# Slot transposes between the second layer's tiles, and the base factors and Gelu's table behind the last routing

## The chip, the cores and the metric

The kernel runs on one core of one Trainium2 chip. The metric is the time of one execution on the device in microseconds (us). Before the change, three runs gave a median of 1468.1 us, from 1467.44 to 1471.71 us. One more execution was recorded by the hardware profiler; every view shown here comes from it.

The engines are named as in the profile: PE is TensorE (PEld its weight loads), DVE is VectorE, ACT is ScalarE, POOL is GpSimd, SP is SyncE, which only issues DMAs here. Each engine works through its own queue in the order in which the program puts instructions there.

## The reference

The input x has 4 batches of 1024 rows with 256 columns. The kernel computes one attention layer and one layer of experts, each followed by a layer norm over x plus the layer's output:

```
x = layernorm(x + attention(x))            # 16 heads of 16, magnitudes by softplus, angles by position
gates = softmax(x @ router_w + router_b)   # 8 experts
mask  = one_hot(top_k(gates, 2)).sum(1)    # two experts for each token
pos   = cumsum(mask, axis=0) - 1           # place of the token in its expert, over all 4096 tokens
valid = mask * (pos < 640)                 # an expert holds 640 tokens, the others get nothing from it
h = gelu(slots @ w1 + b1)                  # 640 x 256 -> 640 x 1024, for each expert
o = h @ w2 + b2                            # 640 x 1024 -> 640 x 256
x = layernorm(x + sum over experts of gates * valid * o)
```

## The kernel before, in words

**Attention and routing.** The attention of all four batches runs first, one pair of heads after another, and takes most of the time. Everything else of a batch, its routing among it, is cut into small pieces that are laid between the pieces of attention. The routing of one batch is a generator, `finish_batch` (L475 to L661); each `yield` ends a piece. It computes the layer norm's factor r (L495 to L502), normalizes rows (L511), transposes them on TensorE (L520), has ScalarE copy them (L525), multiplies by the router's weights (L531), forms gates, the two hot experts, the running count over tokens and the slot of each token (L555 to L629). After that it computes `again`, the factor of a second layer norm for tokens that get no expert's output ("base factors", L633 to L643), and then scatters each tile of 128 rows twice (once for each of the token's two experts) to the slots in DRAM, `slots_in`, by an indirect DMA that GpSimd issues (L652).

**The last routing.** For the last batch there is no attention left to lie beside. L1008 to L1038 run it in two halves of four tiles each, the generators `one` and `two` (with `rotate=True`), whose pieces are interleaved by hand. `one` is run to its end, its scatters included, then the rest of `two`. The base factors of `one` stand therefore on VectorE's and ScalarE's queues ahead of most of `two`.

**The experts.** L1188 to L1264 loop over eight experts; each has 640 slots, which are five tiles (ST = 5) of 128. The order of each engine's work is that of the program (`tc.manual_schedule()`). For each expert e:

- `slots_of(e + 1)` (L1054) queues the load of the next expert's slots on SP. The tile has two buffers, so this load starts when the last reader of the expert two before, the sum at L1163, is done.
- VectorE works out where results go (`tokens_of`, L1070), and the rows of the expert before are normalized (`normalized`, L1116) and sent out (L1176); the partial sums of earlier experts are gathered (L1153) and added (L1163). In the first expert only, `without_experts` (L1137) multiplies all rows by `again` and stores them.
- First layer, L1211 to L1227: eight chunks of the hidden size, each four matrix products on TensorE (L1215; in fp32 the trace shows two matmuls for each) and one Gelu on ScalarE (L1222).
- Second layer, L1228 to L1261: for each of the five tiles t, eight products (16 matmuls in the trace, L1234), then VectorE adds the bias (L1249), ScalarE scales by the gate (L1250), VectorE adds to the running rows (L1251), and GpSimd scatters the result (L1252).
- Ahead of tile t = 3 of the second layer, the slots of the next expert are transposed (`transposed`, L1061 to L1068): two TensorE transposes for each slot tile into PSUM and one ScalarE copy out of it. The PSUM tile `ps_t` has two buffers (L1045), so the transposes of the third slot tile need the copy of the first. The transposed slots `slots_t` have two buffers too.
- After the second layer, the weights of expert e + 2 are queued on SP (L1264).

ScalarE needs a table for its functions. The program loads the one for Sin at L120 and the one for Ln and Exp at L204 by name; the loads for Gelu and for the Sqrt of the last expert are put ahead of the first use by the compiler.

Of the kernel before, what the change touches and what calls it, by code (L numbers as in the profile page):

```python
# [14 lines left out]
AF = mybir.ActivationFunctionType  # L15
ALU = mybir.AluOpType
# [5 lines left out]
EPS = 1e-5  # L22
# [6 lines left out]
def kernel(  # L29
# [18 lines left out]
    nc = tc.nc  # L48
    B, S, DIM = x.shape
    E, _, HID = w1.shape  # L50
    HD = 16
    NT = S // P
# [8 lines left out]
    ST = CAP // P  # L61
# [23 lines left out]
    again = keep.tile([P, B * NT], F32, name="again")  # L85
# [16 lines left out]
    with ExitStack() as actx:  # L102
# [206 lines left out]
        xts, qks, oss, ots, stats = {}, {}, {}, {}, {}  # L309
# [165 lines left out]
        def finish_batch(b, rotate=False, lo=0, n=NT):  # L475


            mv = stats[b][:, lo : lo + n, :]
# [8 lines left out]
            def t1(name):  # L487
                return some(name, (NT,))[:, lo : lo + n]
# [5 lines left out]
            r, v, t = t1("ln_r"), t1("ln_v"), t1("ln_t")  # L494
# [134 lines left out]
            nc.vector.tensor_reduce(  # L629
                held[:, tiles, DIM : DIM + 2].rearrange("p t k -> p k t"), both, AX.X, ALU.add  # L630
            )

            more = again[:, b * NT + lo : b * NT + lo + n]  # L633
            nc.vector.tensor_tensor(v, r, r, ALU.mult)
            nc.vector.tensor_tensor(v, v, mv[:, :, 1], ALU.mult)
            nc.vector.tensor_scalar(v, v, EPS, None, ALU.add)
            nc.scalar.activation(more, v, AF.Ln)
            nc.scalar.activation(more, more, AF.Exp, scale=-0.5)
            yield
            nc.vector.tensor_tensor(t, more, more, ALU.mult)  # L640
            nc.vector.tensor_tensor(t, t, v, ALU.mult)
            nc.vector.tensor_scalar(t, t, -0.5, 1.5, ALU.mult, ALU.add)
            nc.vector.tensor_tensor(more, more, t, ALU.mult)  # L643
            for st in range(n):
                if st:
                    yield
                t = b * NT + lo + st
                if not rotate:

                    nc.vector.tensor_copy(scatter_idx[:, :, t], to[:, :, st])  # L650
                for k in range(2):
                    nc.gpsimd.indirect_dma_start(  # L652
                        out=scatter_views[2 * t + k],
                        out_offset=bass.IndirectOffsetOnAxis(
                            ap=scatter_idx[:, k, t : t + 1], axis=0
                        ),
                        in_=held[:, t, :],
                        in_offset=None,
                        bounds_check=SLOTS - 1,
                        oob_is_err=False,  # L660
                    )  # L661

        zero = aconst.tile([P, ROW], F32, name="zero")
        nc.gpsimd.memset(zero, 0.0)
# [174 lines left out]
        def run(pieces):  # L839
            next(pieces, None)  # L840
# [21 lines left out]
        for b in range(B):  # L862
# [10 lines left out]
            second = ((6, 4), (6, 6), (7, 0), (7, 2))  # L873
# [21 lines left out]
        with tc.manual_schedule():  # L895
# [48 lines left out]
            n = 0  # L944
# [14 lines left out]
        with tc.manual_schedule():  # L959
            for n in range(NS):  # L960
                u, c = divmod(n, NT)
                b, p = divmod(u, NU)
                if c == 0:
                    if u + 2 < B * NU:
                        load_qk(u + 2)
                    elif u + 2 - B * NU < 2:
                        e = u + 2 - B * NU
                        experts[e] = expert_weights(e)
                v, k = divmod(n + 1, NT)
                v, k = v + 1, 2 * k  # L970
# [30 lines left out]
                if b > 0 and (p, c) in FINISH:  # L1001
                    if b not in finishing:
                        finishing[b] = finish_batch(b - 1)
                    next(finishing[b], None)
# [3 lines left out]
        with tc.manual_schedule():  # L1008
            b, n = B - 1, NT // 2
            normalize(B * NU - 1, rotate=True)  # L1010
            for i in range(2):
                turn_back(b, 1, i, rotate=True)
            for j in range(2):
                project(b, 1, j, rotate=True)
                statistics(b, j)
            one, two = (finish_batch(b, rotate=True, lo=lo, n=n) for lo in (0, n))
            run(one)
            project(b, 1, 2, rotate=True)
            for _ in range(3):
                run(one)  # L1020
            project(b, 1, 3, rotate=True)
            for j in range(2, 4):
                statistics(b, j)
            for _ in range(3):
                run(one)
            run(two)
            for _ in range(2):
                run(one)
            run(two)
            for _ in range(4):  # L1030
                run(one)
            run(two)
            for _ in range(3):
                run(one)
            for _ in range(n):
                run(one)
            for _ in two:
                pass  # L1038


    with ExitStack() as mctx:
# [146 lines left out]
        with tc.manual_schedule():  # L1188
            for t in range(ST):
                transposed(0, tiles[0], t)  # L1190
            for e in range(E):
                w1_sb, w2_sb = experts.pop(e)
                s_sb, s_t = tiles.pop(e), s_ts.pop(e)
                if e + 1 < E:
                    tiles[e + 1] = slots_of(e + 1)
                if e == 0:
                    for q in range(7, 3, -1):
                        without_experts(q)
                w, to = tokens_of(e, s_sb)
                others = others_of(e, s_sb, w, to)  # L1200
                row = next(others)

                if before:
                    b_row, b_to = before
                    normalized([b_row[:, t, :] for t in range(ST)], f"e_{e}")
                next(others, None)
                if before:
                    for t in range(ST):
                        sent(b_row, b_to, t)
                h_t = m2.tile([P, HC, CAP], F32, tag="h", name=f"h_{e}")  # L1210
                for c in range(HC):  # L1211
                    ps = ps_h.tile([P, 2, 512], F32, tag="h", name=f"hp_{e}_{c}")
                    for k in range(KC):
                        for i in range(2):
                            nc.tensor.matmul(  # L1215
                                ps[:, i, 0:half],
                                w1_sb[:, k, c * P : (c + 1) * P],
                                s_t[:, k, i * half : (i + 1) * half],
                                start=(k == 0),
                                stop=(k == KC - 1),  # L1220
                            )
                    nc.scalar.activation(  # L1222
                        h_t[:, c, :].rearrange("p (i n) -> p i n", i=2),
                        ps[:, :, 0:half],
                        AF.Gelu,
                        bias=b1_sb[:, e, c : c + 1],
                    )  # L1227
                for t in range(ST):  # L1228
                    if e + 1 < E and t == ST - 2:
                        for i in range(ST):  # L1230
                            transposed(e + 1, tiles[e + 1], i)
                    ps = ps_o.tile([P, DIM], F32, tag="o", name=f"op_{e}_{t}")
                    for c in range(HC):
                        nc.tensor.matmul(  # L1234
                            ps,
                            h_t[:, c, t * P : (t + 1) * P],
                            w2_sb[:, c, :],
                            start=(c == 0),
                            stop=(c == HC - 1),
                        )  # L1240
                    if e == E - 1:
                        nc.vector.scalar_tensor_tensor(
                            row[:, t, :], ps, w[:, t : t + 1], row[:, t, :], ALU.mult, ALU.add
                        )
                        normalized([row[:, t, :]], f"e_{e}_{t}", by_scalar=True)
                        sent(row, to, t)
                        continue
                    o_sb = m4.tile([P, DIM], F32, tag="o", name=f"o_{e}_{t}")
                    nc.vector.tensor_tensor(o_sb, ps, b2_sb[:, e, :], ALU.add)  # L1249
                    nc.scalar.activation(o_sb, o_sb, AF.Identity, scale=w[:, t : t + 1])  # L1250
                    nc.vector.tensor_tensor(row[:, t, :], row[:, t, :], o_sb, ALU.add)  # L1251
                    nc.gpsimd.indirect_dma_start(  # L1252
                        out=y_views[e * ST + t],
                        out_offset=bass.IndirectOffsetOnAxis(ap=to[:, 1, t : t + 1], axis=0),
                        in_=o_sb,
                        in_offset=None,
                        bounds_check=2 * N - 1,
                        oob_is_err=False,
                    )
                    if e == 0 and t < 4:  # L1260
                        without_experts(3 - t)  # L1261
                before = row, to
                if e + 2 < E:
                    experts[e + 2] = expert_weights(e + 2)  # L1264
# [68 lines left out]
```

## Time and profile before

| | us |
|---|---|
| median of three runs | 1468.1 |
| the profiled execution, as timed | 1469.84 |
| its span, first to last instruction | 1468.0 |
| PE busy | 1372.4 (93%) |
| DVE busy | 917.8 (63%) |
| ACT busy | 728.6 (50%) |
| POOL busy | 410.2 (28%) |
| last attention product ends | about 1104 |
| first transposes of expert 0's slots | 1157.26 |
| first layer of expert 0 starts | 1160.05 |
| first layer of expert 7 starts | 1421.09 |

The mean granted clock of TensorE is 0.97 of full speed over the span.

How to read the views. A line of a timeline has the start in us, the duration (of a merged group, its sum of busy time), the engine, the line of the kernel, the operation, what is written and read, the shape, and how many instructions are merged (x64). In square brackets stands the idle time of the engine just before, and the event that ended it: `[0.93 <-issue]` means that the engine stood for 0.93 us and the profile shows no other instruction that released it. A line of the waits has the waiting engine and line, what it waited for, then the total in us, the number of times and the longest. In the slices of the page each digit is the busy share of a fortieth of the span, in tenths; PEclk is the granted clock in the same way. Ends of matmuls are modelled, so starts are the safer numbers.

### The profile page before, as it was taken

What the parts mean: (1) busy time and instruction counts of PE and PEld (TensorE: products, weight loads), DVE (VectorE), ACT (ScalarE), POOL (GpSimd) and SP (SyncE); (2) the same over time, 40 slices, a digit from 0 to 9 for tenths busy, and PEclk for the clock granted to TensorE, in tenths of its full rate; (3) what the DMA queues carried; (4) which work ended last, traced back from release to release, by engine and by line L of the source; (5) the groups of instructions that cost most, each with busy time, mean ns of one, the idle gap of its engine ahead of it and who ended that gap; (6) DMA issues with size and microseconds to landing.
All of it is one profiled execution on the core that took longest, in us unless ns stands there. A gap on an engine that the chain in (4) does not pass through costs nothing. (4 is left out here: it accounts for less than half of the span.)

```text
span 1468.0 us, 24361 instructions
## 1 busy us (share of the span) xinstructions
PE 1372.4 (93%) x9314; PEld 860.1 (59%) x9314; DVE 917.8 (63%) x1990; ACT 728.6 (50%) x944; POOL 410.2 (28%) x436
## 2 busy tenths in 40 slices
PE   5899999999999999999999999999994599999996
PEld 3455556555655565656556555555543377777775
DVE  6767766667877766787766677787715243333334
ACT  5365666565556656555664754655462222222221
POOL 5640043340002646000064520000402224434432
PEclk8799999999999999999999999999996699999998
DMA  7856367374344646453474542243210454333211
GB/s 234 262 161 186 99 189 201 89 226 119 108 120 137 190 128 212 122 153 88 116 216 134 151 135 63 71 105 84 76 58 7 131 181 154 107 115 130 72 40 43
DMA packets 107315, 191.23 MB, mean 130 GB/s; under 512 B 19633, under 2 KB 56178, under 8 KB 107072
## 3 DMA queue, kind: packets, MB, share of 16 engines
q1 hardware_dynamic: 96192, 167.80, 39.6%
q0 software_dynamic: 9888, 20.01, 4.4%
q10 hardware_dynamic: 1120, 1.87, 0.4%
q8 instruction: 73, 1.20, 0.4%
q14 instruction: 42, 0.34, 0.1%
HBM read 119.32 MB, written 73.63 MB: 131 GB/s over the span
## 5 line engine op out<-in xcount | busy, mean ns | idle before, releaser
L692 DVE TENSOR_REDUCE nm<-s 128x1 f32<-128x512 f32 x1024 | 644.6, 683 | 231.7 <-PE s L688 217.3
L737 ACT ACTIVATE pt<-st 128x1024 f32<-128x1024 f32 x512 | 496.2, 1021 | 392.7 <-PE st L730 375.8
L688 PE MATMUL s<-qk 128*128 128x512 f32 x1024 | 390.7, 440 | 23.7 <-DVE nm L692 12.1
L715 PE MATMUL st<-qk 128*128 128x512 f32 x1024 | 308.9, 401 | 4.4 <-ACT pt L737 3.4
L751 PE MATMUL av<-pt,va 128*32 128x256 f32 x4096 | 275.6, 386 | 0.5 <-ACT pt L737 0.5
L688 PEld LDWEIGHTS s<-qk 128*128 128x128 f32 x1024 | 179.9, 191 | 136.6 <-DVE nm L692 58.2
L715 PEld LDWEIGHTS st<-qk 128*128 128x128 f32 x1024 | 182.8, 189 | 68.1 <-ACT pt L737 33.2
L751 PEld LDWEIGHTS av<-pt,va 128*32 128x32 f32 x4096 | 107.2, 109 | 108.2 <-issue 63.0
L652 POOL DMA_INDIRECT slots_in<-held,scatter_idx x64 | 62.6, 977 | 306.0 <-DVE scatter_idx L650 225.1
L390 POOL TENSOR_TENSOR soft_q<-y_q,soft_q 128x512 f32<-128x512 f32 x14 | 17.9, 1279 | 448.0 <-ACT soft_q L386 448.0
L1234 PE MATMUL op<-w,h 128*128 128x256 f32 x640 | 140.6, 379 | 0.0
L1215 PE MATMUL hp<-slots_t,w 128*128 128x320 f32 x512 | 139.8, 434 | 0.0
L1234 PEld LDWEIGHTS op<-w,h 128*128 128x128 f32 x640 | 121.1, 190 | 17.0
L730 PE MATMUL st<-mt,ones_r 2*128 2x512 f32 x1024 | 130.1, 498 | 0.7 <-ACT mt L708 0.7
L1215 PEld LDWEIGHTS hp<-slots_t,w 128*128 128x128 f32 x512 | 97.7, 191 | 39.9 <-ACT slots_t L1068 0.3
L730 PEld LDWEIGHTS st<-mt,ones_r 2*128 2x128 f32 x1024 | 49.2, 182 | 90.0 <-issue 88.6
L1222 ACT ACTIVATE h<-hp,b_sb 128x640 f32<-128x640 f32 x64 | 50.8, 793 | 85.3 <-PE hp L1215 73.0
L1249 DVE TENSOR_TENSOR o<-op,b_sb 128x256 f32<-128x256 f32 x35 | 14.8, 424 | 103.7 <-PE op L1234 99.8
L1250 ACT ACTIVATE o<-o,w 128x256 f32<-128x256 f32 x35 | 17.8, 507 | 109.1 <-DVE o L1249 100.3
L1252 POOL DMA_INDIRECT y_rank<-o,rows x35 | 35.6, 1016 | 109.3 <-ACT o L1250 61.5
L1176 POOL DMA_INDIRECT out_dram<-row,rows x40 | 41.3, 1033 | 44.8 <-DMA out_dram<-row,rows 14.3
L463 DVE TENSOR_TENSOR held<-po,held 128x512 f32<-128x512 f32 x32 | 22.1, 690 | 41.8 <-PE po L455 41.8
(210 smaller groups left out, 1038.3 us busy)
## 6 DMA issues: line engine op xcount, KB each, us to landing
qk<-embed_q SPq DMA_DIRECT2D x248, 128.0 KB
qk<-embed_k SPq DMA_DIRECT2D x124, 256.0 KB
embed_k<-parts_k SPq DMA_DIRECT2D x64, 256.0 KB
w<-in_w_dram SPq DMA_DIRECT2D x16, 1024.0 KB
embed_q<-parts_q SPq DMA_DIRECT2D x56, 256.0 KB
y_rank<-zero SPq DMA_DIRECT2D x8, 1024.0 KB
tab_k<-table SPq DMA_DIRECT2D x14, 512.0 KB
tab_q<-table SPq DMA_DIRECT2D x12, 512.0 KB
```

What stands on the lines that cost most here:

```text
L652: nc.gpsimd.indirect_dma_start(out=scatter_views[2 * t + k], out_offset=bass.IndirectOffsetOnAxis(ap=scatter_idx[:, k, t : t + 1], axis=0) ...
L688: nc.tensor.matmul(ps, qk[:, 2 * h, lo : lo + P], qk[:, 2 * h + 1, j * HS : (j + 1) * HS], start=True, stop=True,)
L692: nc.vector.tensor_reduce(nms[u][:, j, i, s : s + 1], ps, AX.X, ALU.max, negate=True)
L715: nc.tensor.matmul(ps[:, f, :], qk[:, 2 * h + 1, c * P : (c + 1) * P], qk[:, 2 * h, f * HS : (f + 1) * HS], start=True, stop=False,)
L730: nc.tensor.matmul(tiles[h][:, f, :], ones_r[rows, :], mts[u][rows, :], start=False, stop=True,)
L737: nc.scalar.activation(pt, tiles[h], AF.Exp)
L751: nc.tensor.matmul(av[32 * s : 32 * (s + 1), cols], va[f][:, c, 2 * p + h, :], pt[h][:, s // 2, cols], start=(c == 0 and n == 0), stop=(c ...
L1176: nc.gpsimd.indirect_dma_start(out=out_views[t], out_offset=bass.IndirectOffsetOnAxis(ap=to[:, 0, t : t + 1], axis=0), in_=row[:, t, :], i ...
L1215: nc.tensor.matmul(ps[:, i, 0:half], w1_sb[:, k, c * P : (c + 1) * P], s_t[:, k, i * half : (i + 1) * half], start=(k == 0), stop=(k == KC ...
L1222: nc.scalar.activation(h_t[:, c, :].rearrange("p (i n) -> p i n", i=2), ps[:, :, 0:half], AF.Gelu, bias=b1_sb[:, e, c : c + 1],)
L1234: nc.tensor.matmul(ps, h_t[:, c, t * P : (t + 1) * P], w2_sb[:, c, :], start=(c == 0), stop=(c == HC - 1),)
L1252: nc.gpsimd.indirect_dma_start(out=y_views[e * ST + t], out_offset=bass.IndirectOffsetOnAxis(ap=to[:, 1, t : t + 1], axis=0), in_=o_sb, in ...
```

## The change

Three edits. First, the ten transposes for the next expert no longer stand in one group ahead of tile 3. Slot tile 0 is transposed ahead of t = 1, slot tile 1 ahead of t = 2, slot tile 2 ahead of t = 3, and slot tiles 3 and 4 ahead of t = 4. Second, the base factors become a generator of their own, `second_factors`. For the batches that lie beside attention the order stays what it was. For the two halves of the last batch it runs behind the scatters: that of `two` when `two` is run out, that of `one` after it. Third, the table for Gelu is loaded by name right after that.

```diff
@@ finish_batch
-            more = again[:, b * NT + lo : b * NT + lo + n]
-            nc.vector.tensor_tensor(v, r, r, ALU.mult)
-            nc.vector.tensor_tensor(v, v, mv[:, :, 1], ALU.mult)
-            nc.vector.tensor_scalar(v, v, EPS, None, ALU.add)
-            nc.scalar.activation(more, v, AF.Ln)
-            nc.scalar.activation(more, more, AF.Exp, scale=-0.5)
-            yield
-            nc.vector.tensor_tensor(t, more, more, ALU.mult)
-            nc.vector.tensor_tensor(t, t, v, ALU.mult)
-            nc.vector.tensor_scalar(t, t, -0.5, 1.5, ALU.mult, ALU.add)
-            nc.vector.tensor_tensor(more, more, t, ALU.mult)
+            second = second_factors(b, lo, n, r, v, t)
+            if not rotate:
+                next(second)
+            yield
+            if not rotate:
+                next(second, None)
             for st in range(n):
...
+            if rotate:
+                yield
+                for _ in second:
+                    pass
+
+        def second_factors(b, lo, n, r, v, t):
+            more = again[:, b * NT + lo : b * NT + lo + n]
+            nc.vector.tensor_tensor(v, r, r, ALU.mult)
+            nc.vector.tensor_tensor(v, v, stats[b][:, lo : lo + n, 1], ALU.mult)
+            nc.vector.tensor_scalar(v, v, EPS, None, ALU.add)
+            nc.scalar.activation(more, v, AF.Ln)
+            nc.scalar.activation(more, more, AF.Exp, scale=-0.5)
+            yield
+            nc.vector.tensor_tensor(t, more, more, ALU.mult)
+            nc.vector.tensor_tensor(t, t, v, ALU.mult)
+            nc.vector.tensor_scalar(t, t, -0.5, 1.5, ALU.mult, ALU.add)
+            nc.vector.tensor_tensor(more, more, t, ALU.mult)
@@ the last routing
             for _ in two:
                 pass
+            run(one)
+            nc.scalar.preload_act_table_set("gelu_and_others")
@@ the experts' second layer
                 for t in range(ST):
-                    if e + 1 < E and t == ST - 2:
-                        for i in range(ST):
+                    if e + 1 < E and t > 0:
+                        for i in (t - 1,) if t < ST - 1 else (t - 1, t):
                             transposed(e + 1, tiles[e + 1], i)
```

## The prediction

> **What bounds the kernel now.** I read the page's slices first, then the timeline of TensorE alone in the expert stage, then TensorE's waits, then all engines' timeline where the two stages meet. In the slices:
>
> ```profile
> PE   5899999999999999999999999999994599999996
> PEclk8799999999999999999999999999996699999998
> ```
>
> One slice is 36.7 us. TensorE is full everywhere except at the start, in slices 30 and 31 (about 1101 to 1175 us: the last routing), and at the very end. So time is won only by taking something out of TensorE's own queue, or by shortening the chain through slices 30 and 31. TensorE's timeline of one expert (e = 2), with the first line of the next one:
>
> ```profile
> 1235.09 17.39 PE L1215 MATMUL hp<-slots_t,w 128*128 128x320 f32 x64
> 1252.32 10.52 PE L1234 MATMUL op<-w,h 128*128 128x256 f32 x48
> 1262.68 0.60 PE L1067 MATMUL st<-ident,slots 128*128 128x128 f32 x4
> 1264.21 0.71 PE L1067 MATMUL st<-ident,slots 128*128 128x128 f32 x4 [0.93 <-issue]
> 1265.11 0.44 PE L1067 MATMUL st<-ident,slots 128*128 128x128 f32 x2 [0.19 <-ACT slots_t L1068]
> 1265.38 7.07 PE L1234 MATMUL op<-w,h 128*128 128x256 f32 x32
> 1272.29 17.39 PE L1215 MATMUL hp<-slots_t,w 128*128 128x320 f32 x64
> ```
>
> Read the starts. First layer 17.23 us (1252.32 - 1235.09); three tiles of the second layer 10.36, so 3.45 a tile; the ten transposes of the next expert's slots 2.70 (1265.38 - 1262.68); two more tiles 6.91. Together 37.20. In the 2.70 us TensorE stands twice. Its waits from 1178 to 1438 us are only these:
>
> ```profile
> PE st L1067 <- ACT slots_t L1068: 6.7, 12, 0.9
> PE st L1067 <- issue: 1.1, 2, 0.9
> ```
>
> Fourteen waits, two for each of seven experts: the transposes write a ring of two PSUM tiles (ps_t), ScalarE empties them, and its copies stand behind the second-layer output of the tile before. Now the meeting of the stages, in the timeline of all engines:
>
> ```profile
> 1126.62 0.22 DVE L629 TENSOR_REDUCE held<-both 128x8 f32<-128x64 f32 x1
> 1126.76 0.15 DVE L634 TENSOR_TENSOR ln_v<-ln_r 128x4 f32<-128x4 f32 x1
> ...
> 1127.83 0.16 DVE L640 TENSOR_TENSOR ln_t<-again 128x4 f32<-128x4 f32 x1 [0.51 <-ACT again L638]
> ...
> 1128.51 0.97 DVE L511 TENSOR_SCALAR held<-held,mv,ln_r 128x256 f32<-128x256 f32 x2
> 1129.06 1.17 PE L520 MATMUL x1p<-ident,held 128*128 128x128 f32 x4 [3.05 <-DVE held L511]
> 1130.27 0.58 ACT L525 COPY xt<-x1p 128x512 f32<-128x512 f32 x1 [2.00 <-PE x1p L520]
> ...
> 1141.40 0.97 POOL L652 DMA_INDIRECT slots_in<-held,scatter_idx  x1 [4.34 <-DVE ln_v L635]
> ```
>
> From L634 on, VectorE works at the second factors of the first half, which nobody needs yet, while L511 of the second half stands behind them, and TensorE and ScalarE wait for L511. The last line is the first of the second half's eight scatters; GpSimd had been idle for 4.34 us. (The line names L635, but L635 began at 1141.22 and lasted 0.16; L629, done at 1141.12, is 0.28 earlier, the same distance as 1126.84 to 1127.12 in the first half. L629 releases it.) Eight scatters, the load of slots and the first transposes at 1157.26 follow without slack.
>
> **Part 1, the transposes between tiles.** Nothing is added to or removed from TensorE's work: ten transposes stay, in groups of 2, 2, 2 and 4 in place of one group of 10. What goes is the waiting. How long is a group that doesn't wait? In the unstalled first four, narrow windows of the same timeline give starts of 1262.68, 1262.79, 1262.90 and 1263.01: 0.11 each. Entering costs nothing: the two tiles behind give 6.91 / 32 = 0.216 us a matmul, and 48 of them from 1252.32 end where the transposes start. Leaving: the last transposes start at 1265.11 and 1265.27, the matmul after them at 1265.38, so 0.27 for a group of two that came out of a wait. Low bound 10 x 0.11 = 1.10, high bound 5 x 0.27 = 1.35; I take 1.20, nearer to the unstalled row, since these groups come behind full matmuls. Saved: 2.70 - 1.20 = 1.50 for each of six experts and 2.65 - 1.20 = 1.45 for e = 0 (1188.33 to 1190.98), 10.45 in all; bounds 9.4 and 11.1.
>
> Do the waits come back? The ring: transposes of slot tile 2 (at t = 3) need the copy of tile 0, two tiles earlier; those of tile 4 (at t = 4) need the copy of tile 2. That copy comes behind o_2 on ScalarE: VectorE's add ends some 0.6 us after the tile's matmuls, the scale takes 0.51, the copy 0.37, so about 1.6 us after the tile, and the transposes come 3.9 us after it: 2.3 us of cover. The last two copies (two of 0.37) end about 1.9 us into the last tile and the next first layer wants them 3.9 us in. On ScalarE a copy now stands before o_t of each tile; it waits only for transposes at the head of that tile's 3.45 us, so it is through before o_t can start. Uncovered, a late copy costs its lateness.
>
> The slots must be there 6.9 us earlier than now (t = 1, not t = 3). The load is issued when L1163 of the expert before is through: for e = 3 at 1219.73, used at 1262.68. Only the load used in e = 1 is close: issued at 1199.35 among two weight loads; the gathers name it as landed by 1209.17, and t = 1 would want it at 1218.57. Cover 9.4 us; at most it costs what is missing, once.
>
> **Part 2, the second factors.** Off the path of the first half go L634 to L643: seven VectorE instructions and two on ScalarE with 0.51 us of waiting. L511 can start when L629 is issued through, about 1126.81 in place of 1128.51: 1.70 us. ScalarE's Ln and Exp (1127.36, 1127.59), ahead of the first x1p copy, go too; that copy no longer decides. From L511 on each link waits for the one before, so the shift reaches 1141.40. There GpSimd's idle 4.34 us less 1.70 stays positive, so the first half's scatters don't become the limit. I take 1.70, bounds 1.2 and 1.9 (VectorE's row pair took 0.97 here and 0.73 beside an idle GpSimd).
>
> The moved steps issue no DMA and pass no queue of SP or GpSimd. They land behind the second half's own factors, which end at 1142.86, 1141.2 when shifted; 1.8 us more ends at 1143.0. The next VectorE work, L1142, waits for a scatter until 1145.99, 1144.3 shifted: cover 1.3 us, and beyond it only stores of x1 that nobody waits for.
>
> TensorE's clock may take some back. The windows say 0.50 before 1160 and 0.76 in 1160 to 1163: half speed until about 1161.44. That is why the first expert's first layer took 17.92 in place of 17.23. The Trainium skill (TensorE: Matmul & The Clock Gate, Part 4) holds that transposes don't count as busy, which would keep the first layer cold for a whole window of about 3.4 us (Part 1) and cost 1.7 us; the trace had 0.69, 4.2 us after the first transpose, so the row decides. The same Part 1 has the window free-running: by it the warm end falls 3.4 to 6.8 us after the start, 0.3 to 2.0 us lost, -0.4 to +1.3 against now. Shifting the start has no preferred sign; I take 0.
>
> **Part 3, the table.** One load moves from before the first Gelu to behind the last Exp:
>
> ```profile
> 1160.30 0.37 ACT L1068 COPY slots_t<-st 128x256 f32<-128x256 f32 x1 [0.35 <-PE st L1067]
> 1160.69 1.28 ACT L1222 ACT_TABLE_LOAD   x1
> 1163.10 0.79 ACT L1222 ACTIVATE h<-hp,b_sb 128x640 f32<-128x640 f32 x1 [1.13 <-PE hp L1215]
> ```
>
> The skill (ScalarE: Activation LUTs, What ACT_TABLE_LOAD costs) prices a switch at 2.66 us, load and drain; by it I would take off up to 2.66. But the Gelu stood 1.13 us idle after the load, for TensorE: the load lies beside the matmuls, and its removal is worth 0. In its new place ScalarE is idle for 15.92 us, so it costs 0 too; uncovered it would be 1.28. The copies and the Identity between the Gelus cause no load now (the page's groups have four loads in the kernel), so none is added.
>
> **Sum.** 10.45 + 1.70 = 12.15. The profiled span goes from 1468.0 to 1455.85, its execution (1469.84, 1.84 around the span) to 1457.7. The median of runs, 1468.1, is 1.74 below that execution: 1456.0.
>
> **Rivals.** *Switching costs more.* Each exit from transposes exposes the next weight load (0.19): four exits, 0.76 an expert, 5.3 in all: 1461.3. Against it: the exit above took 0.11. *The clock or VectorE eats part 2*: 1457.7. *The wait moves*: transposes find slots or ring not ready and lose what they saved; only part 2 is left, 1466.4. For it: ScalarE's in-order queue; against it the covers above. *Slower, the clock of the dense stage*: the breaks go, TensorE runs without any pause from the first expert on, and its granted clock drops. From 1178 us on some 265 us are TensorE's; the gain is gone at 265 x (1/c - 1) = 12.15, c = 0.956. At 0.93, which the window of 30 to 200 us shows, it costs 19.9: 1475.9. Against it: the windows of 200 to 600 us are 99% busy at 1.00.
>
> **How the numbers follow.** Forecast 0.76; dearer switches 0.10; part 2 lost 0.08; wait moved 0.04; clock 0.02. The forecast's own range: at best 11.1 + 1.9 + 0.4 = 13.4, and the lowest run before lies 0.7 under its median, 1454.0; at worst 9.4 + 1.2 - 1.3 = 9.3, 1458.8. The range 1453.5 to 1460.0 takes in it and the third case, and leaves out some 0.18 (the dearer switches, the wait, the clock, and a little below). A measurement here tells apart about 0.3%, 4.4 us: faster by more holds the first three cases, 0.94; within it the moved wait, 0.04; slower 0.02.
>
> **What would show it.** Expert period 35.7 in place of 37.20, the second layer's starts 3.45 apart plus 0.22 to 0.27; no wait of L1067 on slots_t but the first expert's; L511 of the second half at about 1126.8, first transposes at about 1155.6; one table load near 1143 and none before the Gelu. Wrong if TensorE shows a new wait for slots or st between 1180 and 1440, if the first-layer or op spacing grows (clock), or if the chain at 1126 turns out to be set by another link.

## The result, and the profile after

Six runs of the changed kernel gave a median of 1454.74 us (1452.07 to 1456.68), six of the kernel before 1467.77 (1464.69 to 1471.71). The ratio is 0.9905, with a 95% interval from 0.9893 to 0.9917: 13.9 us faster, between 12.2 and 15.7. The medians differ by 13.0. The profiled execution took 1455.47 us with a span of 1453.6, 14.4 under the span of before.

The slices of the page after:

```profile
PE   5899999999999999999999999999996399999996
PEclk8899999999999999999999999999998599999998
```

A slice is now 36.3 us. The hole is still there, in slices 30 and 31, and the rest is as full as before. What changed inside the full part shows in TensorE's timeline of the same expert, e = 2 (the transposes are L1082 now, the second layer L1249):

```profile
1228.77 17.39 PE L1230 MATMUL hp<-slots_t,w 128*128 128x320 f32 x64
1246.00 3.62 PE L1249 MATMUL op<-w,h 128*128 128x256 f32 x16
1249.45 0.38 PE L1082 MATMUL st<-ident,slots 128*128 128x128 f32 x2
1249.67 3.62 PE L1249 MATMUL op<-w,h 128*128 128x256 f32 x16
...
1260.48 0.60 PE L1082 MATMUL st<-ident,slots 128*128 128x128 f32 x4
1260.91 3.62 PE L1249 MATMUL op<-w,h 128*128 128x256 f32 x16
1264.37 17.39 PE L1230 MATMUL hp<-slots_t,w 128*128 128x320 f32 x64
```

No line has square brackets: nothing waits. A group of two takes 0.22 us from its start to the next matmul (1249.67 - 1249.45), the group of four 0.43. The expert takes 35.60 in place of 37.20. The view of TensorE's waits from 1176 to 1430 us, two lines before, is empty, and the windows of the same stretch give a clock of 1.00 and 35.60 us of busy TensorE in each 35.60.

The view of the waits shows less than this: 0.93 + 0.19 = 1.12 us for the group of e = 2 before, where the starts give 1.60 (2.70 less 1.10). There the fourth transpose started at 1263.01 and counts as busy until 1263.28, so part of a stall is counted as work. The starts tell the whole price.

At the meeting of the stages, in the timeline of all engines:

```profile
1125.76 0.22 DVE L629 TENSOR_REDUCE held<-both 128x8 f32<-128x64 f32 x1
1125.90 0.73 DVE L511 TENSOR_SCALAR held<-held,mv,ln_r 128x256 f32<-128x256 f32 x2
...
1126.45 1.09 PE L520 MATMUL x1p<-ident,held 128*128 128x128 f32 x4 [1.30 <-DVE held L511]
...
1138.07 0.97 POOL L646 DMA_INDIRECT slots_in<-held,scatter_idx  x1 [1.88 <-DVE ln_v L666]
```

L511 starts 0.14 us after the start of L629 (1.89 before), and GpSimd's idle time ahead of the second half's scatters falls from 4.34 to 1.88. The first slot transposes start at 1153.96, 3.30 earlier than before. Not all of that is the edit's, as the runs below show.

The moved factors of the first half did not run where I had put them. In the same timeline (L665 to L674 are the factors, L1157 the scaling of finished rows that each wait for a scatter):

```profile
1139.47 0.15 DVE L665 TENSOR_TENSOR ln_v<-ln_r 128x4 f32<-128x4 f32 x1
...
1142.80 0.35 DVE L1157 TENSOR_SCALAR held<-held,again 128x256 f32<-128x256 f32 x1 [3.18 <-DMA slots_in<-held,scatter_idx]
1143.07 0.15 DVE L666 TENSOR_TENSOR ln_v<-ln_v,mv 128x4 f32<-128x4 f32 x1
...
1145.17 1.28 ACT L1053 ACT_TABLE_LOAD   x1
...
1147.66 0.16 DVE L674 TENSOR_TENSOR again<-again,ln_t 128x4 f32<-128x4 f32 x1
```

They ran on VectorE between the rows of L1157, which each wait for a scatter, and so end at 1147.82 and not at 1143. In kernel.py all seven of the first half's stand ahead of the first L1157; nothing on record says what put them between. Nobody waits for them: ScalarE still idles 8.25 us between the table load and the first copy of slots.

### The profile page after: what moved, and what is told of

Read it like the earlier page. It is cut to its first block, busy times and chain, and to the rows that moved or that the text cites. A ratio compares the mean times of both kernels' runs of the same rounds, so it can differ in the third digit from the quotient of the medians.

```text
span 1453.6 us, 24361 instructions
## 1 busy us (share of the span) xinstructions
PE 1367.7 (94%) x9314; PEld 859.4 (59%) x9314; DVE 921.3 (63%) x1990; ACT 727.5 (50%) x944; POOL 411.2 (28%) x436
## 5 line engine op out<-in xcount | busy, mean ns | idle before, releaser
L1249 PE MATMUL op<-w,h 128*128 128x256 f32 x640 | 144.1, 379 | 0.0
L1249 PEld LDWEIGHTS op<-w,h 128*128 128x128 f32 x640 | 119.4, 190 | 15.9
L396 POOL TENSOR_TENSOR e_k<-soft_k,tab_k 128x512 f32<-128x512 f32 x28 | 35.4, 1286 | 46.3 <-DMA tab_k<-table 45.8
```

What stands on the lines that cost most here:

```text
L1249: nc.tensor.matmul(ps, h_t[:, c, t * P : (t + 1) * P], w2_sb[:, c, :], start=(c == 0), stop=(c == HC - 1),)
```

## The experiments

**Theory.** Part 1 is the removal of TensorE's stalls in the group of ten, 1.6 us an expert; part 2 is VectorE's queue; the table is worth nothing. **Rivals.** The table or the granted clock gave part of it; or the ring of PSUM buffers is not what the transposes waited for.

The attention stage alone moves by several us from execution to execution: its last weighted values start between 1095.71 and 1104.86 in the twelve profiles. A timed ratio carries that along, so for effects of 1 or 2 us I measured stretches inside the profiles. In us: A, from that start to the first half's L629; B, from there to the first slot transposes; C, to the first layer of expert 0; D, that layer; H, how long of D the granted clock stood at half, by the clock's records in the trace; E, the mean period of experts 1 to 6. From the first layer of expert 7 to the end of the span it is 46.9 in all twelve.

| kernel | A | B | C | D | H | E |
|---|---|---|---|---|---|---|
| before | 23.66 | 30.64 | 2.79 | 17.92 | 1.39 | 37.20 |
| changed | 23.37 | 28.20 | 2.80 | 18.05 | 1.65 | 35.60 |
| e1 transposes only | 23.05 | 29.96 | 2.80 | 17.97 | 1.49 | 35.60 |
| e2 factors only | 22.95 | 28.24 | 2.80 | 17.52 | 0.58 | 37.20 |
| e3 table only | 23.38 | 29.99 | 2.80 | 18.89 | 3.34 | 37.20 |
| e4 changed, no table | 23.04 | 28.25 | 2.80 | 19.12 | 3.80 | 35.60 |
| e5 copies first | 23.35 | 28.21 | 2.80 | 18.35 | 2.26 | 36.52 |
| e6 one buffer | 23.04 | 28.24 | 5.10 | 19.66 | 4.91 | 36.96 |
| e7 one each | 23.38 | 28.31 | 5.11 | 18.78 | 2.69 | 35.60 |
| e8 rows early | 23.10 | 26.75 | 2.80 | 17.79 | 1.14 | 35.60 |
| e9 changed, again | 23.39 | 28.20 | 2.80 | 17.87 | 1.29 | 35.60 |
| e10 rows early, again | 22.96 | 27.47 | 2.80 | 17.90 | 1.36 | 35.60 |

D less half of H is 17.21 to 17.23 in eleven of the twelve. The twelfth is e7, with 17.44: its D also holds the two transposes ahead of t = 0, 0.22.

**e1, the transposes alone.** The kernel before with

```diff
-                    if e + 1 < E and t == ST - 2:
-                        for i in range(ST):
+                    if e + 1 < E and t > 0:
+                        for i in (t - 1,) if t < ST - 1 else (t - 1, t):
```

> Only the transposes are spread; the base factors and the table stay as before. If TensorE's waits in the group of ten were the cost: expert period 35.60 as in the changed kernel, no wait of the transposes after the first expert, time 11.0 to 11.2 us under before. If a good part of the gain came from the last routing or the table, it is under 9. The Gelu's table load stands again ahead of the first Gelu and the Gelu's wait for TensorE after it is about 1.1.

Ratio 0.9896 (0.9873 to 0.9919), median 1452.75. Column E is the changed kernel's, B is not. The ratio makes 15.2 us, from 11.9 to 18.6, a little beyond the 11.0 to 11.2 that I expected; the runs of before beside it spread from 1459.85 to 1473.51, and the stretches (9.63 in the six periods, and 1.55 in the first expert's second layer) give 11.18. Part 1 needs nothing of the other two.

**e2, the factors alone.** The kernel before with the generator `second_factors` behind the scatters and `run(one)` at the end; no load by name, transposes in one group.

> Only the base factors are moved behind the scatters; transposes in one group of ten, the table loaded by the compiler ahead of the first Gelu. If VectorE's queue was the cost: L511 of the second half starts about 0.15 us after the last reduction of the first half starts (1.9 us before), from that reduction to the first slot transposes 28.2 us as in the changed kernel (30.6 before), time 1.7 to 2.5 under before, expert period 37.20. If it was the granted clock or a passing wait: 29.5 to 30.6.

Ratio 0.9988 (0.9975 to 1.0001): 1.8 us, between 3.7 and none, so the time alone doesn't show it. Timeline of VectorE and TensorE in it:

```profile
1126.90 0.22 DVE L629 TENSOR_REDUCE held<-both 128x8 f32<-128x64 f32 x1
1127.04 0.73 DVE L511 TENSOR_SCALAR held<-held,mv,ln_r 128x256 f32<-128x256 f32 x2
...
1155.14 3.01 PE L1081 MATMUL st<-ident,slots 128*128 128x128 f32 x10 [17.99 <-DMA slots<-slots_in]
```

B is 28.24. Against what? The profile of before says 30.64, but e1 and e3 have the same code there and say 29.96 and 29.99. The 0.67 between them is one event of that one execution. ScalarE's timelines of before and of e1 show it in the second half's L537, and GpSimd's of e1 shows what is left of the 4.34 us of idle time:

```profile
1130.27 0.58 ACT L525 COPY xt<-x1p 128x512 f32<-128x512 f32 x1 [2.00 <-PE x1p L520]
1132.70 0.27 ACT L537 COPY lt<-lp 128x128 f32<-128x128 f32 x1 [1.85 <-PE lp L531]
```

```profile
1131.56 0.58 ACT L525 COPY xt<-x1p 128x512 f32<-128x512 f32 x1 [2.00 <-PE x1p L520]
1133.31 0.27 ACT L537 COPY lt<-lp 128x128 f32<-128x128 f32 x1 [1.17 <-PE lp L531]
...
1142.01 0.97 POOL L652 DMA_INDIRECT slots_in<-held,scatter_idx  x1 [3.67 <-DVE ln_v L635]
```

From L525 to L537 it is 2.43 in before and 1.75 in e1. So part 2 is worth 29.98 - 28.24 = 1.74, the mean of the two against that of the seven with the factors moved and nothing else in this stretch. What held that one copy is not in the profile.

**e3 and e4, the table.** e3 is the kernel before with `nc.scalar.preload_act_table_set("gelu_and_others")` behind the last routing; e4 is the changed kernel without that line.

> Only the table is loaded by name behind the last routing; all else as before. If the load lay beside matmuls: time within 0.3 us of before, the first Gelu again about 3.05 to 3.2 us after the first layer's start, its wait for TensorE 2.4 to 2.6 in place of 1.13. If a switch costs its load and a drain on the path: 1.3 to 2.7 us faster.

> The changed kernel without the load by name, so that the compiler puts it ahead of the first Gelu. If the load was hidden: as the changed kernel, within 0.3 us in the trace from slot transposes to the second layer (20.85 us). If it was on the path: 1.3 to 2.7 longer there.

e3: 1.0010 (0.9993 to 1.0027), which is between 1 us faster and 4 us slower and so too wide for the 0.3 us that I had named; e4: 0.9911 (0.9888 to 0.9934). Both expectations failed by their numbers in the trace. The stretch that I had named for e4, slot transposes to second layer, took 21.92 and not 20.85. In e3 the first Gelu came 4.01 us after the start of the layer (1155.89 - 1151.88) and waited 3.40, where I had 3.05 to 3.2 and 2.4 to 2.6. ScalarE's timeline of e4 and two windows of it, from the start of the first layer on (the stretch, its length, busy time and count of PE, PEld, DVE, ACT and POOL, then PEclk, the DMA share and GB/s), say why; the last line is e3's first Gelu:

```profile
1153.88 1.28 ACT L1236 ACT_TABLE_LOAD   x1
1157.48 0.79 ACT L1236 ACTIVATE h<-hp,b_sb 128x640 f32<-128x640 f32 x1 [2.33 <-PE hp L1229]
```

```profile
1153.24:1156.24 3.00, 3.00 (x7) 1.97 (x7) 0.28 (x1) 1.66 (x2) 0.00 (x0) 0.50 1.09 384
1156.24:1159.24 3.00, 3.00 (x11) 1.97 (x11) 0.00 (x0) 0.79 (x1) 0.00 (x0) 0.87 0.49 171
```

```profile
1155.89 0.79 ACT L1223 ACTIVATE h<-hp,b_sb 128x640 f32<-128x640 f32 x1 [3.40 <-PE hp L1216]
```

The load was done 2.33 us before the Gelu had anything to read; TensorE ran at half clock for 3.8 us of its layer. e3, which has no load in that place, has nearly the same D (18.89) and a clock that came up nearly as late. The full-clock layer of 17.23 and half of H give 19.13 for e4 and 18.90 for e3; 19.12 and 18.89 were measured. So D moves with the clock, and nothing is left in it for the table's place.

**e5, copies ahead of the scale.** The changed kernel, with the ten transposes in one group behind tile 2's matmuls, so that their copies come ahead of tile 2's scale on ScalarE's queue:

```diff
-                    if e + 1 < E and t > 0:
-                        for i in (t - 1,) if t < ST - 1 else (t - 1, t):
-                            transposed(e + 1, tiles[e + 1], i)
...
+                    if e + 1 < E and t == ST - 3:
+                        for i in range(ST):
+                            transposed(e + 1, tiles[e + 1], i)
                     if e == E - 1:
```

> The changed kernel's routing and table, but the ten transposes stay in one group behind tile 2, and their copies are put on ScalarE's queue ahead of tile 2's scale (before, behind it). If the first of the two waits comes from the copies standing behind the scale and the second from the ring of two PSUM buffers alone: the group takes about 1.85 us (2.70 before, 1.10 spread), expert period 36.35, time 5 to 6 us over the changed kernel. If the ring alone is the cause: 2.6 to 2.7, period 37.1, 10 to 11 over the changed kernel.

Ratio 0.9960 (0.9946 to 0.9975), median 1458.69. TensorE's timeline in expert 1:

```profile
1218.29 0.60 PE L1082 MATMUL st<-ident,slots 128*128 128x128 f32 x4
1219.14 0.71 PE L1082 MATMUL st<-ident,slots 128*128 128x128 f32 x4 [0.24 <-ACT slots_t L1083]
1220.04 0.44 PE L1082 MATMUL st<-ident,slots 128*128 128x128 f32 x2 [0.19 <-ACT slots_t L1083]
1220.31 7.07 PE L1246 MATMUL op<-w,h 128*128 128x256 f32 x32
```

The group stands in the same place of TensorE's queue as before; what differs is ScalarE's order, first the kernel before (expert 2), then e5 (expert 1):

```profile
1263.39 0.51 ACT L1250 ACTIVATE o<-o,w 128x256 f32<-128x256 f32 x1 [2.95 <-DVE o L1249]
1263.80 0.63 ACT L1068 COPY slots_t<-st 128x256 f32<-128x256 f32 x2
```

```profile
1218.71 0.65 ACT L1083 COPY slots_t<-st 128x256 f32<-128x256 f32 x2 [2.65 <-PE st L1082]
1219.61 0.65 ACT L1083 COPY slots_t<-st 128x256 f32<-128x256 f32 x2 [0.25 <-PE st L1082]
```

The first wait is 0.24 in place of 0.93, the second stays 0.19, the group takes 2.02, a little more than the 1.85 that I expected and far from the 2.6 of the ring alone. So of the 1.60 us that spreading saves, 0.68 is the place behind the scale and 0.92 is what is left with the ring of two. My 1.85 was five copies of 0.37 without a pause; in the trace ScalarE waits 0.25 for TensorE in turn, so the two engines wait for each other's tiles. Over seven groups it makes 6.4 us, against the 5 to 6 that I expected. A group of ten with more than two buffers behind it was not run.

**e6 and e7, one PSUM buffer.** Both have `bufs=1` for `ps_t`. e6 keeps the changed kernel's places; e7 puts one slot tile ahead of each of the five tiles:

```diff
-                    if e + 1 < E and t > 0:
-                        for i in (t - 1,) if t < ST - 1 else (t - 1, t):
-                            transposed(e + 1, tiles[e + 1], i)
+                    if e + 1 < E:
+                        transposed(e + 1, tiles[e + 1], t)
```

> The changed kernel with one PSUM buffer for the transposes in place of two. If the buffers' release is what they wait for: nothing at t = 1, 2, 3, where a tile lies between, and at t = 4 a wait of 1.3 to 1.6 us, since the copy of slot tile 3 stands behind tile 3's scale; period 36.9 to 37.2, time 9 to 11 us over the changed kernel; also 1 to 2 us more in the first expert's transposes. If one buffer is enough everywhere: no difference.

> One PSUM buffer, and one slot tile ahead of each of the five tiles, the first ahead of t = 0. If a tile of 3.45 us between covers a copy: no wait of the transposes from the second group on, period 35.60 as in the changed kernel, so one buffer with an even spread does what two do; only the first expert's own transposes take 1 to 2 us more. In the second expert the slots are wanted 3.7 us earlier still (about 17.2 us into the expert; they landed some 11 us in): no wait if that reading is right, up to 5 us once if not.

e6: 1.0005 (0.9994 to 1.0015), the whole gain gone. e7: 0.9926 (0.9899 to 0.9954), median 1454.08. TensorE in expert 1 of e6, at t = 4:

```profile
1227.38 0.38 PE L1082 MATMUL st<-ident,slots 128*128 128x128 f32 x2
1228.91 0.44 PE L1082 MATMUL st<-ident,slots 128*128 128x128 f32 x2 [1.15 <-ACT slots_t L1083]
1229.18 3.62 PE L1249 MATMUL op<-w,h 128*128 128x256 f32 x16
```

The wait came back only where two slot tiles meet, with 1.36 us an expert (36.96 - 35.60). That makes 9.5 us over seven experts; the rest of what is lost against the changed kernel's profile is the first expert's own transposes, 2.3 (column C), and the clock of its layer, 1.6 (column D). e7 has no wait of the transposes between 1180 and 1420 and a period of 35.60: with a tile of matmuls between any two, one buffer does what two do. It also wants the slots of expert 2 17.2 us into expert 1, 3.7 earlier than the changed kernel, and they are there. In both, the first expert's own transposes have no matmuls between them and take 2.3 us longer, a little more than I had expected.

**e8, rows early.** With the factors moved, the next link on VectorE is the second pair of rows. The changed kernel with one more piece of `two` at the same place:

```diff
             for _ in range(4):
                 run(one)
             run(two)
+            run(two)
             for _ in range(3):
                 run(one)
```

> The changed kernel, with the second pair of rows of the second half normalized right after the first pair, ahead of the first half's slot numbers. If VectorE's queue still sets the chain: the second half's path gets 1.4 to 1.9 us shorter and the first half's scatters start 0.2 to 0.5 later; GpSimd's idle between the two sets of scatters, 1.88 in the changed kernel, falls to near 0, and the first slot transposes come 1.2 to 1.6 us earlier: 1452 to 1453.5. If GpSimd's scatters or TensorE set it: under 0.4.

Ratio 0.9906 (0.9880 to 0.9933), median 1453.83. GpSimd's timeline, the last scatter of the first half and the first of the second:

```profile
1135.20 1.02 POOL L646 DMA_INDIRECT slots_in<-held,scatter_idx  x1 [0.30 <-issue]
1136.53 0.97 POOL L646 DMA_INDIRECT slots_in<-held,scatter_idx  x1 [0.30 <-DVE ln_v L666]
```

GpSimd's idle time is down to the 0.30 that lies between any two scatters, and B is 26.75. The first half is delayed by 0.06 us (from its L586 to its L611 it is 1.85, 1.79 in the changed kernel), not by the 0.2 to 0.5 that I expected. From here GpSimd is the limit: sixteen scatters, 1.28 us apart.

**e9 and e10, the changed kernel and e8's again.**

> The changed kernel once more, to see what of its profile repeats. If the parts are as read: from the first half's last reduction to the first slot transposes 28.2 us, expert period 35.60; the first expert's first layer anywhere from 17.5 to 19.3 us, by where TensorE's clock comes up; 12 to 14 us under before.

> The kernel with the second half's rows normalized early, once more and beside the changed kernel. If the 1.45 us that its trace gained are real: again 26.75 from the first half's last reduction to the first slot transposes, and 13 to 16 us under before; if it was one execution's luck: 28.2.

e9 gave 0.9910 (0.9884 to 0.9937) and the changed kernel's stretches to 0.02 in B, C and E. e10 gave 0.9902 (0.9876 to 0.9928); its scatters meet with 0.30 us again, but B is 27.47. SP issued the load of slots 1.10 us after the start of the row scaling beside it, where it is 0.29 in e8 and 0.30 in e9:

```profile
1147.92 3.50 DVE L1158 TENSOR_SCALAR held<-held,again 128x256 f32<-128x256 f32 x13 [1.57 <-DMA slots_in<-held,scatter_idx]
1149.02 0.92 SPq L1072 DMA_DIRECT2D slots<-slots_in  x2
```

This is another single hold that the profile doesn't explain. So e8's version wins 0.7 to 1.45 us in its stretch; the timed intervals of the two kernels overlap and don't show it.

## Why the prediction was right

The forecast was 1456.0, the changed kernel's median 1454.74, and the likeliest case happened: both parts at their price, the table at none. The parts in the traces are 11.18 and 1.74, 12.92 against the 12.15 of the sum.

**Part 1, mechanism right, size 0.7 us low.** The six periods give 9.63 and the first expert 1.55, 11.18 against 10.45. The term that was mis-sized is the group that doesn't wait: I took 1.20, and it is about 1.10 (three times 0.22 and 0.43), the low bound. The row nearer to it was the unstalled one alone; the 0.27 of a group that comes out of a wait had no place in the sum. The covers held: e7 shows that even 3.7 us earlier the slots are there, e6 shows what a missing buffer costs.

**Part 2, right within 0.1 us.** 1.74 against 1.70. The profiles of before and after differ by 2.44 in this stretch; 0.67 of that was the held copy in the profile of before, and I had read it as part of the chain: GpSimd's idle 4.34 was 3.67 in e1. The first slot transposes came at 1153.96 and not at 1155.6; 1.5 of these 1.6 us are the held copy, the attention stage (0.57) and A (0.29), none of them forecast.

**The place of the moved factors, wrong without a cost.** The prediction had them end at 1143.0, ahead of L1142 and its waits. They run between those rows, and the table's load came at 1145.17. Only the spare time of ScalarE and VectorE, larger than I needed, kept this free.

**The table, right.** D holds nothing for it in e3 and e4.

**The clock, an estimate of a bound without a sign, right as such.** D lies between 17.52 and 19.66 in the twelve profiles and follows none of the three edits. Between before and changed it took 0.13, which is luck: by e2 and e4 it could have given 0.4 or taken 1.2. e6, with pauses among its first transposes, is 0.4 above the bound of 2.0 lost.

**The rivals.** Dearer switches: entering and leaving cost nothing that can be seen beside 0.11 for each transpose. The moved wait: none, except where e6 took a buffer away. The clock of the dense stage: 1.00 in each of the six expert windows.

The spans differ by 14.4 as the pages round them. By the starts it is 0.57 from an attention stage that ended earlier, 0.29 in A, 2.44 in B and 11.18 of part 1, less 0.13 in D: 14.35. Without the attention, A and the held copy it is 12.8, close to the 13.0 between the medians.

## What to carry to other kernels

A burst of transposes with a small ring behind it runs no faster than tiles pass between the two engines, and slower still where the copies stand behind other work on their queue. Laid one by one between blocks of matmuls that are longer than a copy and what stands ahead of it (here 3.45 us), the transposes cost only their own issue time, 0.11 us each here, and one buffer is then enough. When a chain is short of time, look at what stands on the in-order queue ahead of the link that others wait for, and move what nobody needs yet behind it. Where one profile is compared with another, check the stretch in a third execution with the same code: here more than a quarter of a stretch's gain was a single hold.

## What the runs showed of the hardware

TensorE's clock came up between 3.4 (e2) and 6.6 us (e4) after the first slot transpose in the ten profiles in which the first transposes are one burst of 2.8 us (C and H added; 4.2 in before, 4.5 in changed). In e6 and e7, with pauses of about 0.5 us among them, it was 10.0 and 7.8. The Trainium skill (TensorE: Matmul & The Clock Gate, Part 1) gives a window of about 3.4 us that is free-running, so that its phase has nothing to do with the start of the kernel, and full clock after at least one busy window. An estimate from it is 3.4 to 6.8 us after steady work begins, which fits the ten; what the window counts in e6 and e7 is not shown. Part 4 of that page has transposes not count as busy in the same way. If these didn't count at all, nothing could come before 3.4 us of the first layer; H is below that in ten of the twelve, 0.58 in e2, so the measurement decides against it here. (The trace names the transposes MATMUL and shows no mode.) On a first layer of 17.23 us at full clock this is worth between 0.3 and 1.9 us from one execution to the next (2.4 in e6).

In stretch B two of the twelve profiles contain a single hold of 0.7 to 0.8 us, on ScalarE in one and on SP in the other, with no event in the trace that explains it. Its cause stays open.
